# Where q's two factors are applied: on ScalarE during Q's projection and on GpSimd in the head loop, in place of one VectorE pass through DRAM

## The chip, the cores and the metric

The kernel runs on one core of one Trainium2 chip. The core has a matrix engine (TensorE, PE in the profile, with its weight loads as PEld), a vector engine (VectorE, DVE), a scalar engine (ScalarE, ACT) and a general one (GpSimd, POOL). SyncE (SP) issues most of the DMA transfers; POOL issues some. The metric is device time in microseconds (us) of one execution, given as the median of several.

## The reference

One transformer block over two sequences of 512 tokens (512 channels, 32 heads of 128). All is float32. What matters here is the attention's first half:

```
x = hidden_states;  xn = layernorm(x)
q = xn @ Wq + bq            # (2, 512, 4096)
k = xn @ Wk + bk
v = xn @ Wv + bv
q = gq * q * rsqrt(mean(q*q, -1) + 1e-6)    # over all 4096 channels of a token
k = gk * k * rsqrt(mean(k*k, -1) + 1e-6)
scores = (q_h . k_h) / sqrt(128)            # per head h
attn = softmax(scores);  out = attn @ v
x = x + layernorm(out @ Wo + bo)
x = x + layernorm(ffn(layernorm(x)))        # base product + 8 gated low-rank experts
```

So q carries two factors besides its bias: a vector over channels (`gq`, and the kernel folds `gk` into it, since q and k meet only in the product) and a scalar per token (`rsqrt` of the mean square over all channels), which is known only when all 32 heads of Q have been projected.

## The kernel before

Q and K are kept with channels on the partitions and tokens along the free axis, so one head of one sequence is a tile of 128x512. The kernel runs in stages, and each engine executes its instructions in the order in which the code records them; only SyncE's transfers are placed by the scheduler.

*Projection of Q, then of K* (`project`, line 196). Eight groups of four heads. Each group is a Strassen-Winograd scheme: seven products of half size (`product`, two accumulating matmuls each), with sums of weight blocks made on POOL (`weight_sums`, line 185) and sums of results made on DVE as they leave the accumulators (lines 249 to 303). A finished head tile goes through `keep_it` (line 230): ACT squares it, POOL adds the square into the running sum `accq` or `acck` (line 238), and SP stores the tile in DRAM (`keptq`, `keptk`, line 239).

*Scaling q* (lines 361 to 389). When Q is complete, the token factors `rqs` are made (lines 410 to 414; the tiles are in the pool `ypool`). During K's projection, `scale_some` is called five times a group by the argument `between`. Each call takes up to two steps: DVE multiplies one head of q by `gqk` (a column) and `rqs[b]` (a tile) at line 382, and SP stores it in a second DRAM tensor, `keptqs` (line 383). The q tiles come in fours from `keptq` (line 377).

*Values* (`values`, line 435): seven products per block again, whose 28 first steps run before the head loop and the rest inside it.

*Head loop* (line 721): 64 turns, i = 2 * head + sequence. In turn i the engines get, in this order: DVE sums the exponentials of turn i-1 (`sums`); DVE subtracts the maximum over keys, `below_top(i)`, line 577; PE makes `scores(i+1)` (line 531, `ps<-qh,kh`) and ACT moves them out (line 532); ACT takes `exponentials(i)` (line 580); every second turn the softmax denominators are inverted and used (lines 563 to 599); PE makes some of the value products (line 460) and of the output projection (line 646), whose sums POOL issues as accumulating DMA transfers (line 653); then `top_of(i+1)`, line 535: DVE folds the four key blocks to one by maxima (lines 541 and 542) and POOL reduces that over the partitions (`partition_all_reduce`, line 544, `top<-m`); last, PE makes `weighted(i)` (line 589). The next turn begins with `scores(i+2)` on PE. `fetch(i+3)` in turn i loads k and q of a later head (lines 504 and 506).

*Tail:* rest of the output projection, residual, feed-forward block, where POOL adds the last residuals (line 944).

Of the kernel before, what the change touches and what calls it, by code (L numbers as in the profile page):

```python
# [9 lines left out]
F32 = mybir.dt.float32  # L10
AF = mybir.ActivationFunctionType
# [3 lines left out]
P = 128  # L15
S = 512
D = 512
H = 32
# [14 lines left out]
def kernel(ctx: ExitStack, tc: tile.TileContext, x, wq, wk, wv, wo, vecs, rows, wbase, gates, bexp, out):  # L33
# [159 lines left out]
        nc.gpsimd.tensor_tensor(s4, a12, s2, ALU.subtract)  # L193
        return [a11, a12, a22] + out

    def project(xTs, sums, w_src, bias, step, name, pools, keep, accs, parts, between=lambda: None):

        G = H // GH
        begun = set()
        parts = {0: parts}
        opened = {}
        two = range(2)

        def load_next(g):  # L210
            if g < G:
                parts[g] = weight_sums(load_w(w_src[:, ts(g, GH * P)], f"w_{name}{g}"), f"{name}{g}")

        def product(g, i, a, x, j, tag=None):
            ps = pt(f"p{i}_{name}{g}_{j}", tag)
            for c in range(2):
                nc.tensor.matmul(ps, a[:, c, ts(j, P)], x[c], start=(c == 0), stop=(c == 1))  # L217
            return ps

        def column(v, g, j):  # L220
            return v[:, g * GH + j : g * GH + j + 1]

        def tile_of(what, g, j):
            return opool.tile([P, 512], F32, tag="o", name=f"{what}_{name}{g}_{j}")

        def head(g, b, j):
            pool, tag = pools[j // 2 if len(pools) > 1 else 0]
            return pool.tile([P, 512], F32, tag=tag, name=f"{name}{b}_{g * GH + j}")

        def keep_it(o, g, b, j):  # L230
            h = g * GH + j
            if b not in begun:
                begun.add(b)
                nc.scalar.activation(accs[b], o, AF.Square)
            else:
                sq = tt(f"sq_{name}{b}_{h}")
                nc.scalar.activation(sq, o, AF.Square)  # L237
                nc.gpsimd.tensor_tensor(accs[b], accs[b], sq, ALU.add)  # L238
            nc.sync.dma_start(out=keep[b, h], in_=o)

        def open_chunk(g, tag=None):
            a11, a12 = parts[g][0:2]
            ps1 = [product(g, 1, a11, xTs[0][0:2], j, tag) for j in two]
            ps2 = [product(g, 2, a12, xTs[0][2:4], j, tag) for j in two]
            u1 = opened[g] = [tile_of("u1", g, j) for j in two]

            def leave():
                for j in two:
                    nc.scalar.activation(u1[j], ps1[j], AF.Identity, bias=column(bias, g, j), scale=1.0)
                for j in two:  # L250
                    o = head(g, 0, j)
                    nc.vector.tensor_tensor(o, ps2[j], u1[j], ALU.add)
                    keep_it(o, g, 0, j)

            return leave

        if len(xTs) < B:
            load_next(1)
            leave = open_chunk(0, "ps")
            second = norm_transposed(xs[1], "a1", "aux")  # L260
            leave()
            xTs.append(second())
            leave = open_chunk(1, "ps")
            sums.extend(token_sums(xTs))
            leave()
        t1, t2, t3, t4 = sums
        for g in range(G):
            if g + 1 not in parts:
                load_next(g + 1)
            a11, a12, a22, s1, s2, s3, s4 = parts.pop(g)  # L270
            if g not in opened:
                parts[g] = (a11, a12)
                open_chunk(g)()
                del parts[g]
            u1 = opened.pop(g)
            between()
            u2 = [tile_of("u2", g, j) for j in two]
            for j in two:
                ps = product(g, 6, s2, t2, j)
                nc.vector.tensor_tensor(u2[j], ps, u1[j], ALU.add)  # L280
            between()
            u3 = [tile_of("u3", g, j) for j in two]
            for j in two:
                ps = product(g, 7, s3, t3, j)
                nc.vector.scalar_tensor_tensor(u3[j], ps, column(step, g, j), u2[j], ALU.add, ALU.add)
            between()
            for j in two:
                ps = product(g, 4, a22, t4, j)
                o = head(g, 0, j + 2)
                nc.vector.tensor_tensor(o, ps, u3[j], ALU.add)  # L290
                keep_it(o, g, 0, j + 2)
            between()
            for j in two:
                ps = product(g, 5, s1, t1, j)
                o = head(g, 1, j + 2)
                nc.vector.tensor_tensor(o, ps, u3[j], ALU.add)
                nc.vector.tensor_tensor(u2[j], ps, u2[j], ALU.add)
                keep_it(o, g, 1, j + 2)
            between()
            for j in two:  # L300
                ps = product(g, 3, s4, xTs[1][2:4], j)
                o = head(g, 1, j)
                nc.vector.tensor_tensor(o, ps, u2[j], ALU.add)
                keep_it(o, g, 1, j)
            yield g

    def attention():
        xTs = [norm_transposed(xs[0], "a0", "aux")()]
        gqk = const.tile([P, H], F32, tag="gqk", name="gqk")
        rqs = [ypool.tile([P, 512], F32, tag="y", name=f"rq{b}") for b in range(B)]  # L310
        rks = [const.tile([P, NT], F32, tag=f"rk{b}", name=f"rk{b}") for b in range(B)]
        keptq = dram.tile([B, H, P, 512], F32, tag="q", name="keptq")
        keptk = dram.tile([B, H, P, 512], F32, tag="k", name="keptk")
# [44 lines left out]
            for k in range(2):  # L358
                nc.sync.dma_start(out=keptwo[g, k], in_=of[k])

        keptqs = dram.tile([B, H, P, 512], F32, tag="qs", name="keptqs")

        scale_steps = []

        def scale_some():
            for _ in range(2):
                if scale_steps:
                    scale_steps.pop(0)()

        def scalings():  # L370

            fours = {}

            def four_of(n):
                g, b = divmod(n, B)
                q4 = fours[n] = wide(f"q4_{b}_{g}")
                nc.sync.dma_start(out=q4, in_=keptq[b, ts(g, GH)].rearrange("h p f -> p h f"))

            def scaled(n, j):
                g, b = divmod(n, B)  # L380
                q, h = fours[n][:, j, :], g * GH + j
                nc.vector.scalar_tensor_tensor(q, q, gqk[:, h : h + 1], rqs[b], ALU.mult, ALU.mult)
                nc.sync.dma_start(out=keptqs[b, h], in_=q)
                if j == GH - 1 and n + 3 < NG * B:
                    four_of(n + 3)

            for n in range(3):
                four_of(n)
            return [lambda n=n, j=j: scaled(n, j) for n in range(NG * B) for j in range(GH)]

        for i in range(2):
            of, to = (v.rearrange("p (g j) -> p g j", j=GH) for v in (vec[:, i, :], steps[:, i, :]))
            nc.vector.tensor_tensor(to[:, :, 0:2], of[:, :, 2:4], of[:, :, 0:2], ALU.subtract)
        sums4 = []
        for g in project(xTs, sums4, wq, bq, steps[:, 0, :], "q", [(qpool, "q")], keptq, accq, weight_sums(wq0, "q0")):
            if g == 0:
                nc.sync.dma_start(out=row, in_=rows.partition_broadcast(P))
            if g == 2:
                nc.vector.tensor_scalar(nbthr, bthr, -1.0, None, ALU.mult)
                nc.vector.tensor_tensor(gqk, vec[:, 3, :], vec[:, 4, :], ALU.mult)  # L400
            if g == NG - 2:
                k_parts = weight_sums(load_w(wk[:, ts(0, GH * P)], "w_k0"), "k0")
            value_sums(g // 2, g % 2)
            if 0 < g <= WG:
                output_sums(g - 1)
            if g < WG:
                load_halves(g)
        for g in project(xTs, sums4, wk, bk, steps[:, 1, :], "k", [(kpool, "k"), (upool, "u")], keptk, acck, k_parts, between=scale_some):
            if g == 0:
                for b in range(B):  # L410
                    ssq = pt(f"ssq{b}")
                    nc.tensor.matmul(ssq, ones, accq[b], start=True, stop=True)
                    nc.scalar.activation(rqs[b], ssq, AF.Sqrt, bias=epst[:, 1:2], scale=1.0 / INNER)
                    nc.vector.reciprocal(rqs[b], rqs[b])
                scale_steps.extend(scalings())

        def key_scales(b):
            ssk = pt(f"ssk{b}")
# [82 lines left out]
        def fetch(i):  # L501
# [1 line left out]
            k = kpool.tile([P, 512], F32, tag="k", name=f"kh{b}_{h}")  # L503
            nc.sync.dma_start(out=k, in_=keptk[b, h])
            q = qpool.tile([P, 512], F32, tag="q", name=f"qh{b}_{h}")
            nc.sync.dma_start(out=q, in_=keptqs[b, h])
            qs[i], kk[i] = q, k

        ss, ms = {}, {}

# [196 lines left out]
        for n in range(28):  # L707
# [3 lines left out]
            if n == 12:  # L711
                for i in range(3):
                    fetch(i)
            if n == 18:
                scores(0)
                top_of(0)
# [4 lines left out]
        for i in range(N):  # L721
# [29 lines left out]
            for task in wo_tasks[i]:  # L751
                leaves(task())
            top_of(i + 1)
            if n4 == 1:
                of_pair = head_sums(c - 1)
            if n4 % 2 == 1 and 0 < c <= 2 * WG:
# [228 lines left out]
```

## Time and profile before

| what | value |
|---|---|
| median of 3 runs | 1315.89 us (1311.62 to 1316.43) |
| span of the profiled execution | 1306.8 us |
| mean granted TensorE clock | 0.996 |
| projection of Q | about 21 to 206 us of the span |
| projection of K | about 206 to 400 us |
| first values, then the head loop | about 400 to 1210 us |
| tail | about 1210 to 1307 us |
| `scores` of turn 0 to `scores` of turn 63 (line 531) | 434.8 to 1198.8 us |
| DVE, scaling q (line 382) | 64 of 1.115 us |
| POOL, maximum over partitions (line 544) | 64 of 1.910 us |

The span runs from the first to the last instruction of one execution; the 9.1 us between it and the median lie around the program or in its spread from run to run. A line of the profile names a source line, an engine, an operation, the tiles (written from read, with buffer numbers left out), the count, the total busy time, the mean of one in ns, and what ended the engine's idle time before it.

### The profile page before, as it was taken

The numbers are of one execution on the slowest core, as the hardware profiler recorded it, in microseconds if no ns is written. First come the engines' busy times: TensorE is split into PE (matmuls) and PEld (weight loads), VectorE is DVE, ScalarE is ACT, GpSimd is POOL, SyncE is SP. The second block draws the span as 40 slices with busy tenths as digits, with TensorE's granted clock in tenths as the row PEclk, the third lists the DMA queues.
The fourth block names the chain that finished last, engine by engine and source line by source line (L and its number), as shares of the span: only waits on it lengthen the run. The fifth ranks groups of instructions, "written<-read, shape, count | busy, mean of one in ns | idle before, by whom it ended". The sixth has DMA issues, their size and how long they took to land.

```text
span 1306.8 us, 11743 instructions
## 1 busy us (share of the span) xinstructions
PE 1281.5 (98%) x3518; PEld 654.9 (50%) x3518; DVE 982.1 (75%) x1208; ACT 541.4 (41%) x746; POOL 496.8 (38%) x382
## 2 busy tenths in 40 slices
PE   7999999999999999999999999999999999999987
PEld 4444444444444444455555555555555555555453
DVE  7565665888765477888787787878778888888865
ACT  5222222322221144344545445454544556555343
POOL 4789897556763011111122222323223233332102
PEclk9999999999999999999999999999999999999999
DMA  7799979699997765534465566576566565643301
GB/s 291 250 321 311 337 278 312 221 335 330 313 341 266 255 189 183 175 129 129 129 173 174 140 191 165 135 196 170 153 162 184 129 169 129 170 97 81 89 1 64
DMA packets 150335, 257.01 MB, mean 197 GB/s; under 512 B 12160, under 2 KB 41728, under 8 KB 150272
## 3 DMA queue, kind: packets, MB, share of 16 engines
q1 hardware_dynamic: 137312, 232.67, 53.2%
q0 software_dynamic: 12096, 22.03, 10.2%
q10 hardware_dynamic: 864, 1.57, 0.3%
q8 instruction: 28, 0.46, 0.1%
q14 instruction: 35, 0.29, 0.1%
HBM read 149.26 MB, written 84.93 MB: 179 GB/s over the span
## 4 chain that ended last, share of the span: by engine, by line
PE 95%; DVE 2%; DMA 1%; ACT 1%; issue 0%; SPq 0%; ACTq 0%
PE ps L531 17%; PE o L589 17%; PE aux L460 15%; PE p_k L217 15%; PE p_q L217 14%; PE aux L646 12%; PE psy L692 2%; PE f L864 1%; DMA w_q<-in_wq 1%; DMA wo<-in_wo 1%; ACT s L580 1%; PE f L920 1%; PE hg L857 0%; PE aux L563 0%; ACT n_f L157 0%
## 5 line engine op out<-in xcount | busy, mean ns | idle before, releaser
L544 POOL PARTITION_ALL_REDUCE top<-m x64 | 122.2, 1910 | 606.6 <-DVE m L542 606.6
L532 ACT ACTIVATE s<-ps,rk 128x512 f32<-128x512 f32 x256 | 175.8, 687 | 308.5 <-PE ps L531 287.3
L589 PE MATMUL o<-s,v 128*128 128x512 f32 x512 | 230.6, 593 | 3.4 <-ACT s L580 3.4
L531 PE MATMUL ps<-qh,kh 128*128 128x512 f32 x512 | 230.2, 592 | 0.0
L531 PEld LDWEIGHTS ps<-qh,kh 128*128 128x128 f32 x512 | 97.3, 190 | 122.5 <-issue 120.8
L589 PEld LDWEIGHTS o<-s,v 128*128 128x128 f32 x512 | 97.0, 190 | 103.8 <-issue 95.7
L550 DVE TRANSPOSE_TENSOR_REDUCE quarters<-s 128x64 f32<-128x2048 f32 x64 | 147.2, 2300 | 0.0
L577 DVE TENSOR_TENSOR s<-s,top 128x2048 f32<-128x2048 f32 x64 | 146.0, 2282 | 0.0
L541 DVE TENSOR_TENSOR m<-s 128x1024 f32<-128x1024 f32 x64 | 78.0, 1219 | 62.0 <-ACT s L532 62.0
L580 ACT ACTIVATE s<-s 128x2048 f32<-128x2048 f32 x64 | 121.7, 1902 | 5.0 <-DVE s L577 5.0
L460 PE MATMUL aux<-w_v,t 128*128 128x512 f32 x256 | 115.8, 596 | 0.0
L646 PE MATMUL aux<-wr,oh 128*128 128x256 f32 x448 | 103.0, 380 | 0.0
L646 PEld LDWEIGHTS aux<-wr,oh 128*128 128x128 f32 x448 | 84.6, 190 | 23.2 <-issue 12.9
L237 ACT ACTIVATE sq_q<-q 128x512 f32<-128x512 f32 x62 | 38.9, 631 | 135.1 <-DVE q L290 68.1
L238 POOL TENSOR_TENSOR accq<-accq,sq_q 128x512 f32<-128x512 f32 x62 | 81.0, 1308 | 36.1 <-ACT sq_q L237 34.1
L238 POOL TENSOR_TENSOR acck<-acck,sq_k 128x512 f32<-128x512 f32 x62 | 86.2, 1394 | 20.6 <-ACT sq_k L237 17.4
L237 ACT ACTIVATE sq_k<-k 128x512 f32<-128x512 f32 x62 | 38.7, 630 | 132.3 <-DVE k L290 65.4
L460 PE MATMUL aux<-w_v,nT_a 128*128 128x512 f32 x192 | 87.5, 596 | 0.0
L217 PE MATMUL p_k<-t,s_k 128*128 128x512 f32 x192 | 85.0, 592 | 0.0
L217 PE MATMUL p_q<-t,s_q 128*128 128x512 f32 x192 | 85.0, 592 | 0.0
L646 PE MATMUL aux<-wr,s_o 128*128 128x256 f32 x336 | 77.4, 380 | 0.0
L460 PEld LDWEIGHTS aux<-w_v,t 128*128 128x128 f32 x256 | 47.6, 190 | 55.0 <-issue 54.3
(185 smaller groups left out, 1713.0 us busy)
## 6 DMA issues: line engine op xcount, KB each, us to landing
keptq<-q SPq DMA_DIRECT2D x64, 256.0 KB, 6.9
q<-keptq SPq DMA_DIRECT2D x16, 1024.0 KB, 6.4
keptk<-k SPq DMA_DIRECT2D x64, 256.0 KB, 6.5
w_v<-keptw SPq DMA_DIRECT2D x32, 512.0 KB, 3.9
keptqs<-q SPq DMA_DIRECT2D x64, 256.0 KB, 6.6
qh<-keptqs SPq DMA_DIRECT2D x64, 256.0 KB, 3.0
kh<-keptk SPq DMA_DIRECT2D x64, 256.0 KB, 2.7
keptv<-o_v SPq DMA_DIRECT2D x64, 256.0 KB, 3.1
```

Source lines behind the costliest of these rows:

```text
L217: nc.tensor.matmul(ps, a[:, c, ts(j, P)], x[c], start=(c == 0), stop=(c == 1))
L238: nc.gpsimd.tensor_tensor(accs[b], accs[b], sq, ALU.add)
L460: nc.tensor.matmul(ps, x[c][:, ts(t, P)], w[:, c, :], start=(c == 0), stop=(c == 1))
L531: nc.tensor.matmul(ps, kk[i][:, ts(k, P)], qs[i], start=True, stop=True)
L532: nc.scalar.activation(s[:, k, :], ps, AF.Copy, scale=rks[b][:, k : k + 1])
L541: nc.vector.tensor_tensor(m, s[:, 0:2, :], s[:, 2:4, :], ALU.max)
L544: nc.gpsimd.partition_all_reduce(ms[i], m[:, 0, :], P, ReduceOp.max)
L550: nc.vector.tensor_reduce(quarters.rearrange("p k j -> p (k j)"), ss[i].rearrange("p k (j r) -> p (k j) r", r=32), AX.X, ALU.add, apply_tr ...
L577: nc.vector.tensor_tensor(s, s, top.unsqueeze(1).to_broadcast([P, NT, 512]), ALU.subtract)
L580: nc.scalar.activation(ss[i], ss[i], AF.Exp)
L589: nc.tensor.matmul(po, vs[b, c][:, k, ts(j, P)], ss[i][:, k, :], start=(k == 0), stop=(k == NT - 1))
L646: nc.tensor.matmul(ps[:, t, :], a, right_of[i, g][:, j, :], start=(j == 0), stop=(j == 1))
```

## The change

ACT multiplies each finished q tile in place by its column of `gqk`, after it has been squared and before it is stored. The pass through `keptqs` goes, with `scale_some` and all calls of `between`. The head loop loads q from `keptq`, and POOL multiplies the tile in place by `rqs[b]` two turns ahead: `scaled(i + 2)` stands after `top_of(i + 1)` in turn i. `gqk` is made ahead of Q's projection, and the tiles `rqs` come from the pool of the normalised inputs (`npool`), at the start of K's projection.

```diff
-    def project(xTs, sums, w_src, bias, step, name, pools, keep, accs, parts, between=lambda: None):
+    def project(xTs, sums, w_src, bias, step, name, pools, keep, accs, parts, factor=None):
...
                 nc.scalar.activation(sq, o, AF.Square)
                 nc.gpsimd.tensor_tensor(accs[b], accs[b], sq, ALU.add)
+            if factor is not None:
+                nc.scalar.activation(o, o, AF.Copy, scale=factor[:, h : h + 1])
             nc.sync.dma_start(out=keep[b, h], in_=o)
...
-            between()
             u2 = [tile_of("u2", g, j) for j in two]
...
-        rqs = [ypool.tile([P, 512], F32, tag="y", name=f"rq{b}") for b in range(B)]
...
-        keptqs = dram.tile([B, H, P, 512], F32, tag="qs", name="keptqs")
-        scale_steps = []
-        def scale_some():
-            for _ in range(2):
-                if scale_steps:
-                    scale_steps.pop(0)()
-        def scalings():
...
-            def four_of(n):
-                g, b = divmod(n, B)
-                q4 = fours[n] = wide(f"q4_{b}_{g}")
-                nc.sync.dma_start(out=q4, in_=keptq[b, ts(g, GH)].rearrange("h p f -> p h f"))
-            def scaled(n, j):
-                g, b = divmod(n, B)
-                q, h = fours[n][:, j, :], g * GH + j
-                nc.vector.scalar_tensor_tensor(q, q, gqk[:, h : h + 1], rqs[b], ALU.mult, ALU.mult)
-                nc.sync.dma_start(out=keptqs[b, h], in_=q)
...
+        nc.vector.tensor_tensor(gqk, vec[:, 3, :], vec[:, 4, :], ALU.mult)
...
-        for g in project(xTs, sums4, wk, bk, steps[:, 1, :], "k", [(kpool, "k"), (upool, "u")], keptk, acck, k_parts, between=scale_some):
+        for g in project(xTs, sums4, wk, bk, steps[:, 1, :], "k", [(kpool, "k"), (upool, "u")], keptk, acck, k_parts):
             if g == 0:
+                rqs = [npool.tile([P, 512], F32, tag="nT", name=f"rq{b}") for b in range(B)]
...
-            nc.sync.dma_start(out=q, in_=keptqs[b, h])
+            nc.sync.dma_start(out=q, in_=keptq[b, h])
             qs[i], kk[i] = q, k
+
+        def scaled(i):
+            if i < N:
+                h, b = divmod(i, B)
+                nc.gpsimd.tensor_tensor(qs[i], qs[i], rqs[b], ALU.mult)
...
+            if n in (15, 21):
+                scaled((n - 15) // 6)
             if n == 18:
                 scores(0)
                 top_of(0)
...
             top_of(i + 1)
+            scaled(i + 2)
```

Q's projection is now called with `gqk` as its last argument.

More of the change, by code (lines that the diff above doesn't have):

```diff
@@ L280, in project @@
                 nc.vector.tensor_tensor(u2[j], ps, u1[j], ALU.add)
-            between()
             u3 = [tile_of("u3", g, j) for j in two]
@@ L285, in project @@
                 nc.vector.scalar_tensor_tensor(u3[j], ps, column(step, g, j), u2[j], ALU.add, ALU.add)
-            between()
             for j in two:
@@ L291, in project @@
                 keep_it(o, g, 0, j + 2)
-            between()
             for j in two:
@@ L298, in project @@
                 keep_it(o, g, 1, j + 2)
-            between()
             for j in two:
@@ L359, in output_sums @@
                 nc.sync.dma_start(out=keptwo[g, k], in_=of[k])
-        keptqs = dram.tile([B, H, P, 512], F32, tag="qs", name="keptqs")
-        scale_steps = []
-        def scale_some():
-            for _ in range(2):
-                if scale_steps:
-                    scale_steps.pop(0)()
-        def scalings():
-            fours = {}
-            def four_of(n):
-                g, b = divmod(n, B)
-                q4 = fours[n] = wide(f"q4_{b}_{g}")
-                nc.sync.dma_start(out=q4, in_=keptq[b, ts(g, GH)].rearrange("h p f -> p h f"))
-            def scaled(n, j):
-                g, b = divmod(n, B)
-                q, h = fours[n][:, j, :], g * GH + j
-                nc.vector.scalar_tensor_tensor(q, q, gqk[:, h : h + 1], rqs[b], ALU.mult, ALU.mult)
-                nc.sync.dma_start(out=keptqs[b, h], in_=q)
[L384 to L389, printed above, removed]
         for i in range(2):
@@ L393, in attention @@
             nc.vector.tensor_tensor(to[:, :, 0:2], of[:, :, 2:4], of[:, :, 0:2], ALU.subtract)
+        nc.vector.tensor_tensor(gqk, vec[:, 3, :], vec[:, 4, :], ALU.mult)
         sums4 = []
-        for g in project(xTs, sums4, wq, bq, steps[:, 0, :], "q", [(qpool, "q")], keptq, accq, weight_sums(wq0, "q0")):
+        for g in project(xTs, sums4, wq, bq, steps[:, 0, :], "q", [(qpool, "q")], keptq, accq, weight_sums(wq0, "q0"), gqk):
             if g == 0:
@@ L399, in attention @@
                 nc.vector.tensor_scalar(nbthr, bthr, -1.0, None, ALU.mult)
-                nc.vector.tensor_tensor(gqk, vec[:, 3, :], vec[:, 4, :], ALU.mult)
             if g == NG - 2:
@@ L414, in attention @@
                     nc.vector.reciprocal(rqs[b], rqs[b])
-                scale_steps.extend(scalings())
         def key_scales(b):
```

## The prediction

> **What bounds the kernel now.** I read the page's first part, the chain, the busy time by stretches, then POOL's and PE's rows in the head loop.
>
> ```profile
> PE 1281.5 (98%) x3518; PEld 654.9 (50%) x3518; DVE 982.1 (75%) x1208; ACT 541.4 (41%) x746; POOL 496.8 (38%) x382
> PE 95%; DVE 2%; DMA 1%; ACT 1%; issue 0%; SPq 0%; ACTq 0%
> ```
>
> Engines' busy time, then the chain that ended last: PE is 95% of it. Next, busy time by stretches (us, then PE, PEld, DVE, ACT, POOL, clock, DMA): the projections of Q and of K, the later head loop.
>
> ```profile
> 21.00:206.00 185.00, 185.00 (x432) 81.92 (x433) 111.46 (x147) 49.36 (x80) 152.11 (x116) 1.00 0.84 291
> 206.00:400.00 194.00, 194.00 (x454) 85.90 (x453) 146.55 (x180) 49.69 (x81) 126.35 (x92) 1.00 0.89 309
> 1010.00:1210.00 200.00, 196.11 (x605) 112.69 (x604) 174.55 (x165) 117.03 (x150) 64.29 (x53) 1.00 0.53 129
> ```
>
> PE has no hole in either projection (185.00 of 185, 194.00 of 194). Whatever the change takes from DVE or DMA there frees nothing on the path. It can only be lost where PE is made to wait, so I looked at what will stand between POOL and PE in the head loop. Rows of the timeline (start, duration):
>
> ```profile
> 780.59 2.08 POOL L544 PARTITION_ALL_REDUCE top<-m  x1 [8.42 <-DVE m L542]
> 782.54 0.92 POOL L653 DMA_DIRECT2D acc<-w  x1
> ...
> 786.27 3.60 PE L531 MATMUL ps<-qh,kh 128*128 128x512 f32 x8
> ...
> 1084.43 1.78 POOL L544 PARTITION_ALL_REDUCE top<-m  x1 [9.06 <-DVE m L542]
> ...
> 1086.00 3.60 PE L531 MATMUL ps<-qh,kh 128*128 128x512 f32 x8
> ```
>
> The new multiply stands behind such a reduction, and the scores shown wait for it. The room is 786.27 - 782.67 = 3.60 us in the first pair, 1086.00 - 1086.21 = -0.21 in the second. Over all 63 such pairs the rooms sum to 139.6 us: 10.63 for turn 0, 2.66 on average in turns 1 to 44 (at least 1.4), 0.65 in turns 45 to 62, where every second one is -0.22.
>
> **POOL's code switch.** In the built changed kernel an instruction without operands stands ahead of every multiply and every reduction of the head loop: 127 such, where before has three in all (ahead of lines 190, 544, 944). In before's trace, by source line (durations min/median/max in ns, first and last start), it shows as
>
> ```profile
> L544 POOLq MODIFY_POOL_CONFIG  x2: 15/15/15, 406.7 to 406.7; - x2
> L190 POOLq MODIFY_POOL_CONFIG  x2: 11/11/11, 1.1 to 1.1; - x2
> L944 POOL TENSOR_TENSOR z<-z,y x7: 1262/1269/1282, 1286.9 to 1299.9; 128x512 f32<-128x512 f32 x7
> 10.50 1.27 POOL L190 TENSOR_TENSOR s_q<-w_q 128x512 f32<-128x512 f32 x1 [9.62 <-DMA w_q<-in_wq]
> qh<-keptqs SPq DMA_DIRECT2D x64, 256.0 KB, 3.0
> ```
>
> So POOL is reconfigured when it goes from the reduction to an ordinary multiply and back. The 11 to 15 ns are the sequencer's; what POOL needs behind them is hidden each time, since a long wait follows. I bound it: at least 0.03 us (two records), at most 9.4, since the first switch at 1.10 was over by 10.50, when the multiply started 0.07 us after its input landed. Call it R. I take R = 6.0: a reconfiguration is nearest to a load from DRAM, the row next to it in this stage is qh with 3.0 us from issue to landing, and each switch has two records, 2 x 3.0. The ends 0.03 and 9.4 stay for the range. The GPSIMD Engine Reference of the Trainium skill (Instruction dispatch) says that the first call after a library load waits about 6 us for code without a visible instruction; no run here shows that yet, and by its 5.95 the sum below would be 3 us less.
>
> **Head loop, step by step.** Scores(i+2) start at the earliest at the reduction's end + R + 1.27 (the multiply; L944, 128x512 with both inputs in SBUF) + 0.23 (0.08 from one POOL instruction to the next as in L190's rows, the rest for the semaphore): R + 1.5. Everything up to the next reduction hangs on these scores, so the rooms above don't change, and each turn loses R + 1.5 less its room where that is positive. At R = 6.0 all turns but the first lose: 62 x 7.5 - (139.6 - 10.6) = **+336 us**. Behind the waiting scores PE holds up the denominators, the value and output products and weighted(i+1); ACT and DVE wait for those. The switch back lies beside the scores, their eviction and the maxima (6.5 or 9.0 us from scores to reduction, every second turn). With one or two issues of line 653 (0.9 each) behind the multiply it fits, or is up to 1.2 late in about 23 turns: 0 to 28, taken 0, as the clock term stretches that same part.
>
> The clock: PE then idles 336/62 = 5.4 us a turn. In before, holes of 0.85 us left the clock at full; the one of 3.19 did not (PE's timeline, then clock over its surroundings):
>
> ```profile
> 1268.56 1.09 PE L914 MATMUL hT<-ident,hw 128*128 128x128 f32 x4 [3.19 <-DVE hw L903]
> 1260.00:1276.00 16.00, 12.78 (x62) 0.79 0.01 1
> ```
>
> The mean of 0.79 is 6.83 us at half clock, of which 6.0 fell on work. Scores at half clock cost 3.43 more a turn, on the same chain: 0 to 62 x 3.43 = 213. 5.4 lies beyond 3.19, but the half clock is not tied to the start of a hole, so I take half: **+106**. TensorE: Matmul & The Clock Gate (Part 1) says that the clock halves after an idle window of about 3.4 us. Windows at random phase would lie wholly in 59% of such holes, and the term would be an estimated 125 rather than 106.
>
> **Q's projection.** ACT gets 64 more passes of 128x512, SBUF to SBUF with a column operand, priced as L599 (0.716): 45.8 us on an engine busy for 49.4 of 185. Each store on SP waits 0.7 to 1.4 longer, with the weight loads queued behind it, and tiles of the pool of five come free later: DVE already waits there for a store (L303, 12.4 us in five waits, the longest 4.1). PE does not feel it, as it runs up to eight products of 1.72 ahead. Cost 0; if that cover were gone, 16 groups' waits x 0.72 = 12.
>
> **K's projection.** DVE loses 64 x 1.115 = 71 us, SP's queue 16 loads of 1 MB and 64 stores of 256 KB. PE ran throughout: gain 0, and at most the 3.4 us of PE's holes in the later head loop (four of 0.85), if those were to close. `gqk` ahead of Q, the other pool of `rqs` (its slots' last reader is long past): 0. The 64 multiplies are 81 us more of POOL; that they can hold up a DVE instruction with two SBUF inputs (L625 took 1.41 beside a reduction, L624 0.69) lies behind R, in PE's new holes: 0.
>
> **Sum:** 1306.8 + 336 + 106 = 1749 of span, + 9.1 from span to median = 1758; I say **1755**.
>
> **The rivals.**
>
> *The switch is cheap (R up to 2.7).* For it: its records are 15 ns, no DMA queue of the profile shows a load for it, and ScalarE's own table loads take 1.28 us in the trace. Against: an instruction that needs no time would not be needed. At 1.28 the rooms leave 41 turns late, +59: 1375. At 2.7 (kh's landing) +132, 1448.
>
> *The switch is dearer, and POOL is the bound.* A turn then takes a reduction 1.91 + R + 1.5 + 1.2 (line 653) + R. At 9.4 that is 23.4 against 12.0 now: 62 x 11.4 = +707, 2020. It decides from R = 7.5, where the switch back no longer fits. Against: the first switch would have ended at the very moment its input landed.
>
> *Not slower.* The switch costs its 15 ns alone, and the multiply starts before the reduction's record ends, as line 653's did by 0.12 to 0.15 us. Then turns 1 to 44 have room (at least 1.4 against 1.35), and only the nine late rooms of -0.22 lose, 1.5 each; four holes of 0.85 give back 3.4, the emptier K stage at most the same again. It decides in the late turns and needs R under 0.1: 1316 + 14 - 7 = 1323, the edge of no change. That DVE's relief alone makes it faster would need PE to have waited for DVE, and it did not.
>
> *The change does not do what it says.* All 64 multiplies and 127 switches are in the built program, and the pass is gone: left out.
>
> **How the numbers follow.** The forecast's own case (R 2.7 to 7.5, with the clock between nothing and its full price) has 0.77: 1450 to 1950. Cheap switch 0.11; POOL as the bound 0.08; not slower 0.04. Low: 1440, the cheap case's top. High: 1950, R = 7.4 and scores wholly at half clock (1306.8 + 423 + 213 + 9 = 1952). About 0.2 stays outside. A measurement of this kernel tells about 0.5% from no change (its three runs spread by 0.37%). Faster by more needs a path that no row shows: 0.01; within 0.5%: the not-slower case, 0.03; slower 0.96.
>
> **What would show it.** In the changed kernel's trace: two switch records ahead of each line of the multiply and of the reduction; the multiply starting R after the reduction's end with its input landed; the idle time of `scores` put down to POOL, some 5 us a turn; turns of 17 to 19 us in both halves of the head loop instead of 12.7 and 10.3; half clock in parts of it; Q's and K's projections as long as before. I am wrong if the multiply follows the reduction within 2 us (cheap), if the reduction rather than the scores waits for the switch (dear), or if PE waits in Q's projection.

## The result, and the profile after

The changed kernel takes 1854.06 us (median of 4 runs, 1848.58 to 1862.44), the kernel before on the same chip 1313.76 us (4 runs, 1308.59 to 1316.43): a ratio of 1.413, 95% interval 1.408 to 1.419. The predicted 1755 us lay 5% under it, with 1854 inside the range of 1440 to 1950. What follows compares the two profiled executions, with spans of 1306.8 and 1860.7 us, 553.9 apart (the medians differ by 540).

Engines' busy time on the page of after, the granted clock in its 40 slices, and the shares of the chain that ended last:

```profile
PE 1435.1 (77%) x3518; PEld 700.3 (38%) x3518; DVE 919.0 (49%) x1144; ACT 587.0 (32%) x810; POOL 576.0 (31%) x446
PEclk9999999999888888888888888887887788877899
PE 65%; issue 19%; POOL 6%; DVE 5%; DMA 3%; ACT 1%; SPq 0%; POOLq 0%; ACTq 0%; DVEq 0%
```

PE runs as many matmuls as before, but is busy for 77% of the span instead of 98%, and its own time has grown by 154 us although its work has not: that is the clock. Nothing else is busier than half the time. 19% of the chain is "issue", an engine that waits for nothing the profile can name. The groups of instructions say which engine that is (busy time and mean ns, then the idle time just before them and what ended most of it):

```profile
L502 PE MATMUL ps<-qh,kh 128*128 128x512 f32 x512 | 371.3, 891 | 392.8 <-POOL qh L478 392.8
L478 POOL TENSOR_TENSOR qh<-qh,rq 128x512 f32<-128x512 f32 x64 | 80.1, 1252 | 456.1 <-issue 456.1
```

Line 502 is the scores, 478 the new multiply. PE waited 392.8 us for the multiply. The multiply itself is 64 x 1.25 us, as priced, but POOL sat idle for 456.1 us ahead of it, about 7 us each time, without waiting for data. By source line (durations min/median/max in ns, first and last start), this is what stands in that idle time:

```profile
L478 POOLq MODIFY_POOL_CONFIG  x126: 98/98/98, 453.5 to 1742.0; - x126
L515 POOLq MODIFY_POOL_CONFIG  x128: 1/662/676, 415.1 to 1751.9; - x128
```

Two records of the code switch for each change from the reduction (line 515) to the multiply, and two for each change back. Each record is under 0.7 us, and no DMA queue in the trace carries anything for it (the instruction queues have 65 packets, 63 before). One turn late in the loop (start, duration, engine, line, idle time before):

```profile
1516.89 1.80 POOL L515 PARTITION_ALL_REDUCE top<-m  x1 [9.96 <-DVE m L513]
1526.62 1.25 POOL L478 TENSOR_TENSOR qh<-qh,rq 128x512 f32<-128x512 f32 x1 [7.92 <-issue]
1527.83 1.95 POOL L624 DMA_DIRECT2D acc<-w  x2
1527.93 5.21 PE L502 MATMUL ps<-qh,kh 128*128 128x512 f32 x8 [9.35 <-POOL qh L478]
```

The reduction ends at 1518.69. The multiply's input landed long ago, yet it starts at 1526.62, 7.93 later. It ends at 1527.87, and the scores start at 1527.93, after 9.35 us in which PE had nothing to do. The eight products then take 5.21 us instead of the 3.60 before. By stretches (us, then PE, PEld, DVE, ACT and POOL busy, clock, DMA share, GB/s), after shows Q's projection, K's, and the two parts of the head loop:

```profile
21.00:206.00 185.00, 184.36 (x433) 81.64 (x433) 106.35 (x143) 89.28 (x138) 142.03 (x108) 1.00 0.73 255
206.00:400.00 194.00, 187.66 (x433) 82.55 (x432) 83.50 (x114) 54.80 (x86) 124.23 (x99) 0.98 0.48 169
435.00:1200.00 765.00, 561.02 (x1334) 275.03 (x1333) 371.35 (x383) 218.70 (x273) 146.48 (x106) 0.85 0.36 107
1200.00:1750.00 550.00, 358.20 (x884) 185.53 (x882) 251.37 (x240) 163.90 (x208) 128.59 (x99) 0.81 0.30 76
```

The projections are nearly as full as before. (The end of Q's reaches past 206 now, so its hole counts in the second stretch.) PE is busy for 73% and 65% of the head loop, at clocks of 0.85 and 0.81.

The whole difference by stage, from four points of each profile (the last product of K, the scores of turn 0, those of turn 63, the end):

| stage | before, us | after, us | difference |
|---|---|---|---|
| to the end of K's projection | 400.5 | 411.1 | +10.6 |
| from there to the scores of turn 0 | 34.2 | 34.2 | 0.0 |
| scores of turn 0 to those of turn 63 | 764.0 | 1305.0 | +541.0 |
| tail | 108.0 | 110.3 | +2.3 |

A turn lasts 20.7 us on average (12.1 before), and almost the same in both parts of the loop: 20.83 in turns 1 to 44, 20.52 in turns 45 to 62 (12.72 and 10.30 before). So PE's work no longer sets the turn. A chain does. Its pieces, averaged over turns 1 to 62:

| piece of the turn | us |
|---|---|
| scores' first product to the reduction's start (8.02 before) | 10.29 |
| reduction | 1.92 |
| reduction's end to the multiply's start | 7.23 (median 7.07) |
| multiply | 1.25 |
| multiply's end to the next scores' first product | 0.055 |

They add up to the turn of 20.7. The 541 us thus come from two of them: 7.23 + 1.25 + 0.055 = 8.54 us between reduction and scores, less the room that was there, 62 x 8.54 - 129 = 401; and 62 x (10.29 - 8.02) = 140 for the slow clock. From the trace's clock records, half clock was granted in 64 stretches of 461 us together (13.7 us before); 61 of these, 444 us, lie in the loop: practically one in every turn.

### The profile page after: what moved, and what is told of

Read it like the earlier page. It is cut to its first block, busy times and chain, and to the rows that moved or that the text cites. A ratio compares the mean times of both kernels' runs of the same rounds, so it can differ in the third digit from the quotient of the medians.

```text
span 1860.7 us, 12080 instructions
## 1 busy us (share of the span) xinstructions
PE 1435.1 (77%) x3518; PEld 700.3 (38%) x3518; DVE 919.0 (49%) x1144; ACT 587.0 (32%) x810; POOL 576.0 (31%) x446
## 4 chain that ended last, share of the span: by engine, by line
PE 65%; issue 19%; POOL 6%; DVE 5%; DMA 3%; ACT 1%; SPq 0%; POOLq 0%; ACTq 0%; DVEq 0%
PE ps L502 20%; PE p_k L217 10%; PE aux L426 10%; PE o L560 9%; PE aux L617 7%; PE p_q L217 5%; POOL qh L478 4%; DMA keptq<-q 2%; PE psy L663 1%; DVE oh L569 1%; DVE r L541 1%; PE f L838 1%; DVE m L512 1%; DVE m L513 0%; ACT s L551 0%
## 5 line engine op out<-in xcount | busy, mean ns | idle before, releaser
L502 PE MATMUL ps<-qh,kh 128*128 128x512 f32 x512 | 371.3, 891 | 392.8 <-POOL qh L478 392.8
L502 PEld LDWEIGHTS ps<-qh,kh 128*128 128x128 f32 x512 | 142.9, 294 | 618.1 <-POOL qh L478 444.1
L478 POOL TENSOR_TENSOR qh<-qh,rq 128x512 f32<-128x512 f32 x64 | 80.1, 1252 | 456.1 <-issue 456.1
L538 DVE RECIPROCAL inv<-aux 128x32 f32<-128x32 f32 (+1 forms) x32 | 11.3, 354 | 296.3 <-PE aux L534 296.3
L238 POOL TENSOR_TENSOR acck<-acck,sq_k 128x512 f32<-128x512 f32 x62 | 78.6, 1268 | 63.4 <-ACT sq_k L237 62.6
L434 DVE TENSOR_TENSOR o_v<-aux,u_v 128x512 f32<-128x512 f32 x64 | 43.5, 685 | 97.4 <-PE aux L426 79.7
```

Of the source, the lines that this page charges most:

```text
L478: nc.gpsimd.tensor_tensor(qs[i], qs[i], rqs[b], ALU.mult)
L502: nc.tensor.matmul(ps, kk[i][:, ts(k, P)], qs[i], start=True, stop=True)
```

## The experiments

My theory: a switch of POOL's code costs about 7 us there and something near it back; the half clock follows from the idle time; and the projections lose their 10.6 us to ScalarE's pass or to Q's slots. The rivals: the multiply itself is what is slow or is waited for; the time belongs to any wait on POOL; the switch costs time in one direction only, or in proportion to the instruction behind it; and the clock is a cause of its own. Each edit is to the changed kernel unless it says otherwise. A time without an interval is of a single run; a median with an interval is of repeated runs.

| kernel | time, us | before on the same chip, us | ratio (95%) | turn, us |
|---|---|---|---|---|
| multiply on VectorE | 1318.75 | 1310.35 | 1.0068 (1.0053 to 1.0083) | 12.13 |
| no multiply | 1319.05 | 1310.35 | 1.0073 (1.0057 to 1.0090) | 12.13 |
| multiply ahead of the reduction | 1673.27 | 1310.35 | one run | 17.66 |
| matmuls that keep PE awake | 1771.92 | 1310.35 | one run | 19.36 |
| two multiplies every second turn | 1576.69 | 1308.83 | one run | 16.18 |
| before, with a 128x1 addition | 1625.41 | 1308.38 | one run | 16.92 |
| both factors in one VectorE instruction | 1308.48 | 1308.83 | 0.9994 (0.9985 to 1.0004) | 12.13 |
| multiply on VectorE, more slots for Q | 1308.94 | 1308.83 | 0.9998 (0.9987 to 1.0009) | 12.13 |
| neither factor | 1309.11 | 1308.83 | 1.0001 (0.9992 to 1.0010) | 12.13 |

**The multiply on VectorE.** It undoes only the choice of engine:

```diff
-                nc.gpsimd.tensor_tensor(qs[i], qs[i], rqs[b], ALU.mult)
+                nc.vector.tensor_tensor(qs[i], qs[i], rqs[b], ALU.mult)
```

> The changed kernel with the head loop's multiply by the RMS factor on VectorE in place of GpSimd, same place in the code. If the code switch between the multiply and the reduction on GpSimd is the cost (theory), the head loop goes back to 12.1 to 12.3 us a turn: 1314 plus the 10.6 us by which the projections ended later in the changed kernel, plus 0 to 10 in the late turns, 1320 to 1336. If a q that must first be loaded and multiplied is late on any engine (rival), it stays above 1700.

Measured 1318.75 us (1318.17 to 1319.45), just under the expectation. The multiplies by source line, and the two parts of the loop:

```profile
L478 DVE TENSOR_TENSOR qh<-qh,rq x64: 679/684/686, 438.6 to 1206.3; 128x512 f32<-128x512 f32 x64
```

```profile
450.00:1010.00 560.00, 560.00 (x1583) 297.31 (x1583) 470.21 (x498) 264.35 (x329) 128.55 (x90) 1.00 0.58 167
1010.00:1210.00 200.00, 196.59 (x602) 112.28 (x601) 187.43 (x184) 115.18 (x147) 69.76 (x55) 1.00 0.54 133
```

PE is full again (560.00 of 560), the clock is 1.00, the turn is the 12.13 us of before. All 541 us of the head loop hang on the multiply being on POOL. What stays is 8.4 us, and K's last product at 412.1 us of the span against 400.5.

**No multiply.** Leaves out q's RMS factor:

```diff
-                nc.gpsimd.tensor_tensor(qs[i], qs[i], rqs[b], ALU.mult)
+                pass
```

> The changed kernel without the multiply by the RMS factor (q keeps its channel factor only; the softmax is of other scores). What is left is the new ScalarE pass in Q's projection and the loads from the first store. Theory: 1314 + 10.6 = 1325 (1320 to 1330), all of the difference before the head loop. If the loads or the emptier K stage matter in the head loop, its turns differ from 12.13 us.

1319.05 us (1318.04 to 1321.19), just under the expectation, K's last product at 411.6. So VectorE's 64 multiplies are free in the head loop, and the 8 to 9 us that remain are lost in the projections, where the multiply plays no part.

**The multiply ahead of the reduction.** Here the scores hardly wait for the switch there any more (PE waits 27.6 us in all for the multiply, 392.8 in the changed kernel), but the reduction now waits for the switch back:

```diff
-            top_of(i + 1)
             scaled(i + 2)
+            top_of(i + 1)
```

> The multiply for turn i+2 is issued ahead of the reduction for turn i+1 instead of behind it; the number of switches is the same. Scores no longer wait for a multiply that has just been released, but the switch back to the reduction's code now stands in front of each reduction. If each direction costs what the one in the trace costs (7.1 us), GpSimd is the bound with 1.25 + 7.1 + 1.9 + 1.0 + 7.1 = 18.4 us a turn, some 1720. If the switch back is free, about 11.3 a turn of GpSimd, which is under PE's 12.1: 1325 to 1370.

One run: 1673.27 us. POOL and DVE rows of one turn:

```profile
1315.25 1.06 POOL L624 DMA_DIRECT2D acc<-w  x1
...
1321.94 0.69 DVE L513 TENSOR_TENSOR m<-m 128x512 f32<-128x512 f32 x1
...
1323.50 1.26 POOL L478 TENSOR_TENSOR qh<-qh,rq 128x512 f32<-128x512 f32 x1 [7.18 <-DVE m L513]
1330.54 1.80 POOL L515 PARTITION_ALL_REDUCE top<-m  x1 [5.78 <-issue]
1332.37 2.29 DVE L548 TENSOR_TENSOR s<-s,top 128x2048 f32<-128x2048 f32 x1 [7.22 <-POOL top L515]
```

The switch back is 5.78 us here, 6.0 in the median of 62 turns (5.69 to 8.33); the switch there keeps its 7.15 ("DVE m" is the wait that ended last before it by the profile, but the 7.18 us of idle time recur in every turn). The maxima that the reduction reads are made by 1322.63, so the reduction comes 7.91 us late, and the subtraction of line 548 behind it. POOL does nothing but switch and work: 1.25 + 6.0 + 1.80 + 1.35 (issues of line 624) + 7.15 = 17.6, the measured turn of 17.66. So both directions cost, back somewhat less than the 7.1 I had put in, and the rival in which back is free falls (it asked for 1325 to 1370). POOL is the bound of this kernel, no longer a chain through PE.

**Matmuls that keep PE awake.** The changed kernel with seven extra products of k with itself ahead of the scores. They write the bank that the scores write anew, so what they change is PE's idle time and clock:

```diff
+                if k == 0 and i > 1:
+                    for _ in range(WARM):
+                        nc.tensor.matmul(ps, kk[i][:, ts(k, P)], kk[i], start=True, stop=True)
```

> The changed kernel with seven extra products (k by k, overwritten by the first scores) ahead of each turn's scores, about 6 us of PE work in the hole in which PE waits for the multiply. Theory: the half clock on the scores is 2.26 us of each turn; with the hole filled the clock stays at full and a turn takes 18.4 instead of 20.7: 1854 - 140 = 1714 (1700 to 1740). If the half clock is not on the chain of the turn, the time stays at 1854 or grows.

One run: 1771.92 us, not the 1700 to 1740 expected. It gained 82 us, not 140. The clock rose from 0.877 to 0.986, and half clock in the loop shrank from 444 to 38 us; the scores take 3.95 us instead of 5.82. But the way from the scores to the reduction is 8.63, not the 8.02 of before, the switch there 7.33, and the scores follow the multiply after 0.28. 62 x (1.66 - 0.10 - 0.23) = 82: the gain of the way to the reduction, less what the two others lost. About 0.35 of the missing 0.6 us is the scores, which met the half clock still in ten turns, nine of them after 1330 us. The rest is the switch back: in 12 turns the reduction starts 1.0 to 2.0 us after the maxima that it reads, and 5.8 to 6.6 us after POOL's instruction before it, so that over all turns it starts 0.42 us after the maxima on average (0.17 before). PE's timeline of one of the ten turns, with a hole that the extra products did not close, and then the clock over the scores (columns as for the stretches above):

```profile
1403.47 6.17 PE L505 MATMUL ps<-kh 128*128 128x512 f32 x14
1412.23 5.40 PE L506 MATMUL ps<-qh,kh 128*128 128x512 f32 x8 [2.59 <-POOL qh L479]
```

```profile
1412.00:1417.00 5.00, 4.76 (x7) 2.03 (x8) 0.00 (x0) 1.56 (x3) 2.09 (x3) 0.66 0.61 105
```

Line 505 is the extra products, 506 the scores. A hole of 2.59 us was here followed by a clock of 0.66 and scores of 5.40 us. So the clock term is shown to be a consequence of the idle time, at least 82 of its 140 us by taking it away; the switch there stays, at 7.33 us, with PE awake.

**Two multiplies every second turn**, 63 switches instead of 127 by the records in the traces. Three multiplies stand ahead of the loop, then:

```diff
-            scaled(i + 2)
+            if i % 2 == 1:
+                scaled(i + 2)
+                scaled(i + 3)
```

> The changed kernel with two multiplies behind each other in every second turn, so half as many switches (64 instead of 127). Theory: only every second scores waits for a switch; of a pair of turns one takes about 20.7 + 0.0 and the other 10.3 to 13.9: 31 x (20.7 - 12.1) = 267 less, some 1590 (1560 to 1640). If it is the multiply on GpSimd and not the switch that costs, it stays at 1850.

One run: 1576.69 us, near the 1590 expected. POOL and PE over one pair of turns:

```profile
1200.93 1.80 POOL L515 PARTITION_ALL_REDUCE top<-m  x1 [9.20 <-DVE m L513]
...
1202.46 3.60 PE L502 MATMUL ps<-qh,kh 128*128 128x512 f32 x8
...
1208.95 2.06 POOL L515 PARTITION_ALL_REDUCE top<-m  x1 [4.36 <-DVE m L513]
...
1217.87 2.48 POOL L478 TENSOR_TENSOR qh<-qh,rq 128x512 f32<-128x512 f32 x2 [6.86 <-issue]
...
1219.17 6.49 PE L502 MATMUL ps<-qh,kh 128*128 128x512 f32 x8 [6.23 <-POOL qh L478]
```

Two reductions in a row have no switch between them, and the scores between them run at once, in 3.60 us. The two multiplies also stand without a gap (2.48 for two). Only the change of kind costs, 6.86 here. Half as many switches cost 256 us in the head loop, against 541 in the changed kernel: the price goes with the number of switches, not of multiplies.

**The kernel before, with one addition of 128x1 on POOL** after the reduction of each turn. Nobody reads its result, and q is scaled as before:

```diff
+        idle = const.tile([P, 1], F32, tag="idle", name="idle")
+        nc.vector.memset(idle, 0.0)
...
             top_of(i + 1)
+            nc.gpsimd.tensor_tensor(idle, idle, idle, ALU.add)
```

> The kernel before (q scaled on VectorE in K's stage) plus one addition of 128x1 on GpSimd behind each turn's reduction, of which nothing waits. Theory: the switch is the price, not the multiply and not the wait of scores: GpSimd needs 0.1 + 6.0 (back) + 1.9 + 1.4 + 7.1 (there) = 16.5 us a turn against PE's 12.1, and the reductions come late: 1309 + 62 x 4.4 = 1582, with half clock in some turns up to 1640. If the cost hangs on the size of the multiply or on its place ahead of scores, 1309 to 1325.

One run: 1625.41 us, 317 over the kernel before. The additions by source line, then POOL's timeline (in this kernel line 546 is the reduction, 655 the accumulating DMA):

```profile
L756 POOL TENSOR_TENSOR idle<-idle x64: 182/183/842, 475.1 to 1536.6; 128x1 f32<-128x1 f32 x64
```

```profile
1305.00 1.80 POOL L546 PARTITION_ALL_REDUCE top<-m  x1 [6.16 <-issue]
1313.62 0.50 POOL L756 TENSOR_TENSOR idle<-idle 128x1 f32<-128x1 f32 x1 [6.82 <-issue]
1314.07 1.95 POOL L655 DMA_DIRECT2D acc<-w  x2
1323.55 1.80 POOL L546 PARTITION_ALL_REDUCE top<-m  x1 [7.52 <-issue]
```

64 instructions of 0.18 us that no one waits for make the kernel 24% slower, because POOL's next reduction comes behind two switches (back 6.13 in the median of 62). That is the clearest run of all: it is neither the multiply's size, nor its data, nor a wait of the scores, but the alternation of the two kinds on POOL.

**Both factors in one VectorE instruction.** No pass on ScalarE, no second trip through DRAM, and in the head loop what the kernel before did in K's projection:

```diff
-                nc.gpsimd.tensor_tensor(qs[i], qs[i], rqs[b], ALU.mult)
+                nc.vector.scalar_tensor_tensor(qs[i], qs[i], gqk[:, h : h + 1], rqs[b], ALU.mult, ALU.mult)
```

> The changed kernel without the ScalarE pass in Q's projection; VectorE applies both factors in the head loop in one instruction (column and tile), at the place of GpSimd's multiply. If the ScalarE pass makes the projections end later (theory), they end as before (PE's last product of K at 400.5 us of the span instead of 411 to 412) and the time is that of before, within 0.3%. If the loss comes from what the scheduler does with SyncE's queue once the second store is gone (rival), 1318 as with the ScalarE pass.

1308.48 us (1307.21 to 1309.21; 12 runs), a ratio of 0.9994 to the kernel before, from 0.9985 to 1.0004. K's last product is at 400.6, as before. The chain's shares, then the multiplies' group:

```profile
PE 95%; DVE 2%; ACT 1%; issue 0%; DMA 0%; ACTq 0%
```

```profile
L478 DVE SCALAR_TENSOR_TENSOR qh<-qh,gqk,rq 128x512 f32<-128x512 f32 x64 | 47.7, 745 | 0.0
```

Without the pass Q's projection has no hole. And the trip through DRAM that is gone (16 loads of 1 MB, 64 stores) buys nothing: PE is 95% of the chain with and without it.

**The multiply on VectorE, with ScalarE's pass, and more slots for Q.** This tells whether ScalarE is too slow for the pass or the slots come free too late: besides the edit of the first experiment, Q's projection may take slots of a pool that is idle there:

```diff
-        for g in project(xTs, ..., "q", [(qpool, "q")], keptq, ...):
+        for g in project(xTs, ..., "q", [(qpool, "q"), (upool, "u")], keptq, ...):
```

> The changed kernel with the multiply by the RMS factor on VectorE, and in Q's projection the result tiles of the third and fourth head of a group from the pool u, which is idle then: 12 slots instead of 5, the ScalarE pass stays. If PE's hole of 6 us at the end of Q's projection comes from slots that come free late (theory), it goes: about 1311, within 0.3% of before but for 1 to 2 us at the start, where the pass stands ahead of a copy. If ScalarE is itself too slow for the pass, 1318 as without the slots.

1308.94 us (1308.56 to 1309.89; 12 runs), a ratio of 0.9998 (0.9987 to 1.0009). The hole is gone. Where it was, the changed kernel shows this (ScalarE's pass on one tile, SP's queue, DVE, PE; then its waits, in us in total, times, longest):

```profile
205.22 0.72 ACT L240 ACTIVATE q<-q,gqk 128x512 f32<-128x512 f32 x1
...
217.13 3.13 SPq L241 DMA_DIRECT2D keptq<-q  x4
...
225.53 0.69 DVE L300 TENSOR_TENSOR q<-p_q,u_q 128x512 f32<-128x512 f32 x1 [10.70 <-DMA keptq<-q]
...
226.28 3.78 PE L217 MATMUL p_k<-t,s_k 128*128 128x512 f32 x4 [6.11 <-DVE q L300]
```

```profile
DVE q L300 <- DMA keptq<-q: 52.1, 7, 11.1
```

DVE wants a tile of Q's pool of five and waits 10.70 us until the store of an earlier one has landed. The pass on that tile ended at 205.94, its store was issued at 217.13 and landed at 225.41: 11.2 us in SP's queue behind other transfers and 8.3 on the way, beside which the 0.72 us of the pass are little. What keeps the store in the queue so long no run tells. PE runs out of work for 6.11 us, with 6.83 us at half clock from 223.70 on. With the extra slots the stretch from 206 to 400 us is full again, at full clock:

```profile
206.00:400.00 194.00, 194.00 (x454) 85.97 (x453) 88.76 (x118) 54.35 (x85) 119.22 (x95) 1.00 0.44 159
```

Neither this kernel nor the one without the pass has any wait of line 300 for such a store: without the pass five slots are enough, and with it twelve are.

**Neither factor.** Leaves out both factors on q: no pass and no multiply anywhere.

> The changed kernel without either factor on q (the softmax is of other scores): neither the ScalarE pass nor the multiply. Theory: as before or up to 4 us under it, since the chain is PE's and only its 3.4 us of holes in the head loop could close; rival (the moved stores and loads themselves cost): 1318 and more.

1309.11 us (1307.34 to 1310.07; 10 runs), 1.0001 of the kernel before (0.9992 to 1.0010). Leaving all the work on these factors out gains nothing here, so moving it elsewhere had nothing to gain either. No version that I ran beats the kernel before by more than the interval of its ratio.

## Why the prediction was right, step by step

*POOL's code switch* was right, as a mechanism and as the item on which the time hangs: the multiply starts R after the reduction's end with its input landed. R was taken as 6.0 and is 7.23 on average (median 7.07). With the multiply's 1.25 and 0.055 in place of the allowed 1.5, the term is 401 instead of +336; this is the largest error of the sum, 65 us. How I came to 6.0, "2 x 3.0" of a load's landing, is not shown by any run: no DMA queue shows such a load. That 6.0 came near in size was luck; the bounds of 0.03 and 9.4, which were read from the trace, held.

The rule quoted there, about 6 us for code without a visible instruction (the Trainium skill, GPSIMD Engine Reference, Instruction dispatch), agrees with the 6.0 us of the switch back; the switch to the multiply is above it at 7.07 in the median of 62 turns, and the measurement decides.

*The rooms.* "Each turn loses R + 1.5 less its room": right. With the measured pieces in it, the sum of rooms gives the loop's time to within 1 us (401 + 140 against 541).

*The switch back*, taken as 0 of 0 to 28: right. In the changed kernel the reduction starts 0.21 us after the end of the maxima, 0.17 before. It fits because the scores, slower now, give it room: in the run that keeps PE awake it is 1.0 to 2.0 us late in 12 turns, and where it has no room, with the multiply ahead of the reduction, it costs its full 6.0.

*The clock*, taken as +106 of 0 to 213: 140 measured, 34 us more. I halved the full price since the half clock need not fall on the scores; with holes longer than I had (PE waits 392.8 / 62 = 6.3 us for the multiply alone, not 5.4) it fell on them in nearly every turn, for part of their length: 5.82 us of scores between the 3.60 at full clock and the 7.03 at half.

*Q's projection*, "PE does not feel it, as it runs up to eight products of 1.72 ahead": this step failed. Products can be ahead only as far as DVE takes them off, and DVE stopped for up to 11.1 us at a time. Nor did a store start 0.7 to 1.4 us later: the one shown above stood 11.2 us in the queue after its pass. The price I gave for the lost cover, 12 us, was the one that applied: 8.4 us in the times of the run on VectorE, 10.6 in the spans. A row that could have warned was in the prediction, five waits of together 12.4 us for the same store, already in the kernel before, in a pool of five:

```profile
L303 DVE TENSOR_TENSOR q<-p_q,u_q 128x512 f32<-128x512 f32 x16 | 11.1, 692 | 20.6 <-DMA keptq<-q 12.4 <-PE p_q L217 4.8 <-ACT sq_q L237 3.4
```

In the changed kernel the same wait is 52.1 us in seven. A wait that is hidden by little is not cover for more of the same.

*K's projection*, "gain 0": right, and shown by the two runs at 1308.5 and 1308.9, which do without the trip through DRAM and win nothing.

*The rivals.* The cheap switch falls with 7.23 us where it allowed 2.7, and "not slower" with it; the time of before comes back only with the multiply off POOL, as on VectorE with more slots for Q. The dearer one, POOL as the bound "from R = 7.5", was missed narrowly: in no turn of the changed kernel does the reduction wait for the switch. The multiply ahead of the reduction made POOL the bound at R of 7.15 and 6.0, since there neither direction has cover.

*Sum.* Of the span's 553.9, predicted 442: 65 of the 112 missing are R, 34 the clock, 10.6 Q's projection, 2.3 the tail. A turn was to take 17 to 19 us and takes 20.7. The 9.1 us added from span to median were too many: every run's time is some 1.8 us above its own span, so a span of 1306.8 us belongs to a time near 1308.6, the low end of that kernel's spread.

## What to carry to other kernels

An engine with idle time is not free for any work: look at what stands before and after the new instruction on it, and count the changes of kind, since on POOL every change between the reduction over partitions and an elementwise multiply or addition cost some 6 to 7 us in these runs, for an instruction of 128x1 as for one of 128x512. In a profile this shows as idle time put down mostly to "issue", with two configuration records at the line of the next instruction; batch one kind, as the run with pairs did for half the cost, or put the work on another engine, as VectorE took it for 0.68 us. And before removing work, ask whether anything on the path waits for it: here nothing did, and the best that any of these placings reached was a tie.

## What the hardware showed that I had not expected

The two directions of the switch differ: 7.07 to 7.29 us from the reduction to the elementwise operation, 6.0 to 6.13 back (medians over 62 turns; the first in the changed kernel, with the multiply ahead of the reduction and with the 128x1 addition, the second in the latter two). What these microseconds consist of no record shows.

The clock halves with less idle time than I had seen. In the kernel before, the only hole that was followed by half clock was of 3.19 us. With the extra matmuls, holes of 2.59 us (at 1409.65) and 2.03 us (at 1505.04) were followed by half clock from 1412.86 and 1508.44, for 3.41 us each by the clock's records. Of PE's holes in that loop all eight of 2.31 us and more were followed by half clock, two of the four of 2.03 to 2.22 us, and none of the 21 of 0.67 to 1.74 us. The Trainium skill (TensorE: Matmul & The Clock Gate, Part 1) speaks of an idle window of about 3.4 us; the step agrees with that length, but such a window need not be idle from end to end. What share of it must be idle these runs don't tell.
